# A windowed-attention and convolution kernel: buffers reused in the conv's tail, the next stage's first loads and table load placed among its last steps, and the depthwise taps loaded by channel

## The chip, the cores and the metric

The kernel runs on one core of a Trainium2 chip. A core has five engines, each with its own queue of instructions: TensorE (PE, matrix products), VectorE (DVE), ScalarE (ACT), GpSimd (POOL) and SyncE (SP, which here only issues transfers). ACT and POOL issue transfers too. The metric is the device time of one execution in microseconds (us); the median of several executions is compared.

## The reference

The input is `x`, 4 images of 128 channels and 128x128 pixels, fp32. Two layers follow one another.

```python
# layer 0
tok = regions(x)                     # 9x9 regions of 16x16 pixels, step 14, per image
y = ln(tok); q, k, v = split(y @ w_qkv)           # 4 heads of 32
o = softmax(q k^T / sqrt(32)) v
merged = overlap_average(o @ w_out + b_out + tok)
xf = merged.reshape(b, h * w, c)
y = ln(xf) @ w_p0 + b_p0                          # 256 channels
ym = depthwise_conv5x5(y, dw_k)                   # dw_k: [256, 1, 5, 5]
ym = batch_norm(ym)                               # statistics over all 4 images
y = gelu(gelu(ym)) @ w_p2 + b_p2 + xf
# layer 1
out = conv3x3(act_quant(y), weight_quant(w1)); out = batch_norm(out)
out = conv3x3(act_quant(out), weight_quant(w2)); out = batch_norm(out)
return out + y
```

The batch norms split the work: the gelu stage can't begin before the depthwise conv of the whole batch has its statistics.

## The kernel before, in words

**Stages.** The first, long stage (to about 2134 us) does attention, the first projection and the depthwise conv. Then comes the gelu stage (`gelu_stage`, L1228), which works through 64 units of 1,024 pixels: two gelus, second projection, residual, quantisation, first 3x3 conv. The second 3x3 conv (`last_stages`, L1354) ends the kernel.

**First stage.** An image is cut into 9 bands of regions, 36 bands in all; a band has 9 regions. For each region PE makes scores (L829), ACT exponentials (L837), DVE and POOL the sums `sm` of the two halves of the keys (L847), PE the weighted values (L892) and the sums (L900); DVE takes reciprocals (L912) and products `part` (L914, L916), and POOL adds regions into the band's output `ob` (L919). When a band is complete, `post_begin` (L545 to L557) averages the seams of `ob` on POOL; then `post_chunks` works on the band in chunks of 8 rows or fewer: the output projection (`product`, L473), the residual `xf` on DVE (`project`, L584), the second layer norm (squares L406, sums by PE L412, statistics L418 to L427), the first projection and its eviction `y` by ACT (L602), and stores of `y` to DRAM. The layer norm's row is spread over the partitions by a DRAM round trip (`xn<-row`, L446), except in the last band, where four selector matrices `sel` (made at L391) do it on PE (L439).

**Order.** PE, ACT, DVE and SP keep the order in which the program issues; POOL's instructions are placed by a scheduler and then run in order. `beside(t)` gives, for each of the 9 regions of band `t`, lists of small jobs of other bands. A list of single steps, `todo`, is dealt out over the first bands in the same way: it makes the matrices of the depthwise conv. The conv itself is a product with banded matrices: `zeros` loads the 25 taps of 256 channels as [25, 256] (L241), clears a scratch tile and stores it over `pad_d` in DRAM (L243), `padded_taps` writes the taps into it (L254), `by_outputs` reads bands out of it with a skewed pattern (L263), and later steps turn them and store them to `dw_d`. The second step after `padded_taps` is empty. When the list is done, `clear` (L322) zeroes the three input tiles `ut_` of the conv; the three weight tiles `wt_` are zeroed at the start. Their empty places stay zero after that.

**The conv.** `depthwise` (L640) multiplies weight tiles `w` (loaded from `dw_d`, L629) with input tiles `u` (loaded from `y2_d` by `fill`, L654: the main part by SP, two halo rows by POOL). Images 0 to 2 and the first half of image 3 are done beside the attention. The second half of image 3 is the tail: `conv_rest` (L733) runs 16 steps with a ring of six buffer pairs `ur`, `wr`, which it allocates and zeroes first (L750 to L757). It issues the weight loads and most of the input loads for six steps; after the last band's chunks, `run_all` loads the remaining rows and runs the steps. Each step has two results, which ACT copies out of PSUM (L769), DVE takes statistics of (L773), and SP and ACT store to `cv_d` (L776).

**Between the stages.** DVE and POOL work out scale and shift of the batch norm (`affine`, L1051). `gelu_stage` opens its pools, SP issues the loads of units 0 and 1 (`load` L1241 and L1246, `load_xf` L1255), and ACT runs the gelus (L1263, L1266), whose function table is loaded when the first of them comes up.

Of the kernel before, what the change touches and what calls it, by code (L numbers as in the profile page):

```python
# [14 lines left out]
P = 128  # L15
# [33 lines left out]
def layers(  # L49
# [135 lines left out]

    with ExitStack() as actx:
        pool = lambda name, bufs, **k: actx.enter_context(
            tc.tile_pool(name=f"{name}_{tag}", bufs=bufs, **k)  # L190
# [30 lines left out]
        def scratch(n):  # L221

            return turned(ut_)[:, :n]
# [6 lines left out]
        def band_matrices():  # L230

            held = {}

            def zeros():
                zero = scratch(28 * CW)
                nc.gpsimd.memset(zero, 0.0)
                held["taps"] = taps = scratch(2 * P)[:N_TAPS]  # L240
                nc.sync.dma_start(out=taps, in_=dw_k.rearrange("c o i j -> (o i j) c"))  # L241
                n = (2 * GR + 3) * 7 * 2 * P // P
                nc.sync.dma_start(  # L243
                    out=pad_d.rearrange("y x c -> (y x c)").rearrange("(p n) -> p n", p=P),
                    in_=zero[:, :n],
                )
                held["zero"] = zero

            def edge(b, m, n, g):
                nc.gpsimd.dma_start(  # L250
                    out=rows_in(b, g, m, n), in_=held["zero"][:, : n * CW].rearrange("p (n x) -> p n x", x=CW)
                )

            def padded_taps():  # L254
                for dy in range(5):
                    nc.sync.dma_start(
                        out=pad_d[GR - 1 + dy, 1:6, :], in_=held["taps"][5 * dy : 5 * dy + 5, :]
                    )

            def by_outputs(ro):  # L260
                for eo in range(2):

                    nc.sync.dma_start(  # L263
                        out=band_d[2 * ro + eo].rearrange("s (r e) c -> r s (e c)", e=2),
                        in_=bass.AP(
                            pad_d.tensor,
                            pad_d[GR - 1 - ro, 1 - eo, 0:1].offset,
                            [[7 * 2 * P, GR + 4], [4 * P, 3], [1, 4 * P]],
                        ),
                    )  # L270

            def load(c, s):
                by_m = scratch(32 * 64)[:KD].rearrange("p (m c) -> p m c", m=32)
                nc.sync.dma_start(
                    out=by_m, in_=band_d[:, s, :, c : c + 64].rearrange("m p c -> p m c")
                )
                held[c, s] = by_m

            def turn(c, s, half):
                if half == 0:  # L280
                    held["c"] = scratch(32 * 64)[:KD]
                by_m, by_c = held[c, s], held["c"]
                nc.vector.tensor_copy(
                    by_c[:, half * 1024 : half * 1024 + 1024].rearrange("p (c m) -> p m c", m=32),
                    by_m[:, :, 32 * half : 32 * half + 32],
                )
                if half:
                    del held[c, s]
                    h, k = divmod(c // 16, NCK)
                    for m, d in enumerate(dw_d):  # L290
                        n = d.shape[2] // 2
                        for jj in range(2):
                            nc.sync.dma_start(
                                out=d[k : k + 4, jj, n * h : n * h + n, 256 * s : 256 * s + 256].rearrange(
                                    "k p n -> p k n"
                                ),
                                in_=by_c[2 * GR * m : 2 * GR * m + n].rearrange(
                                    "p (k j n) -> p k j n", j=2, n=8 * 32
                                )[:, :, jj],
                            )  # L300

            def several(*steps):
                def run_all():
                    for s in steps:
                        s()
                return run_all

            each = lambda f, args: [lambda a=a: f(*a) for a in args]
            pieces = [(c, s) for c in range(0, 2 * P, 64) for s in range(3)]
            steps = [zeros, padded_taps, lambda: None]  # L310
            edges = [
                (b, 2 * GR * half + m, n, g)
                for b in range(B) for half in range(2)
                for m, n, g in ((0, 4, 0), (4, 4 if b == B - 1 else 28, NG - 1))
            ]
            for ro in range(GR):
                steps.append(several(*each(edge, edges[ro : ro + 1]), lambda ro=ro: by_outputs(ro)))
            steps += [lambda: None, lambda: load(*pieces[0])]

            def clear():  # L320
                for t in ut_:
                    nc.gpsimd.memset(t, 0.0)  # L322


            for n, p in enumerate(pieces):
                steps.append(
                    several(lambda p=p: turn(*p, 0), *each(load, pieces[n + 1 : n + 2]))
                )
                steps.append(lambda p=p: turn(*p, 1))
            steps.append(clear)  # L330
            return steps
# [398 lines left out]
                for half in range(2)  # L730
            ]

        def conv_rest(n, pool):  # L733

# [10 lines left out]
                U[at], W[at] = ring[at % ahead]  # L747
                weights(W[at], *tiles[at], nc.gpsimd.dma_start)

            ring = []  # L750
            for n_ in range(ahead):
                ring.append((
                    pool.tile([P, ng, 8, CW], F32, name=f"ur{n_}"), pool.tile([P, 3, 8, 32], F32, name=f"wr{n_}"),
                ))
                for t, engine in zip(ring[-1], (nc.vector, nc.gpsimd)):
                    engine.memset(t, 0.0)

            for at in range(ahead):
                begin(at)
# [3 lines left out]
            def step(at):  # L763
# [1 line left out]
                pc = score_banks(at, ng)  # L765
                depthwise(pc, W[at], U[at], 8)
                for half in range(2):
                    cv = pool.tile([P, 2, ng, CW], F32, name="cr", bufs=8)
                    nc.scalar.copy(  # L769
                        cv.rearrange("p j g x -> p (j g x)"), pc[half].rearrange("p j g x -> p (j g x)")  # L770
                    )
# [9 lines left out]
            def run_all():  # L781
# [3 lines left out]
                for at in range(len(tiles)):  # L785
                    step(at)
                    if at % 2:
                        chunk_stats(at // 2)
                    if at + ahead < len(tiles):
                        begin(at + ahead)  # L790
                        load(at + ahead, 0, ng)

            return run_all

# [213 lines left out]
        with nullcontext() if safe else tc.manual_schedule(engines=MANUAL):  # L1008
# [26 lines left out]
            post_begin(T - 1)  # L1035

            bctx.close()
            late = actx.enter_context(tc.tile_pool(name=f"late_{tag}", bufs=1))
            assert not todo
            run(left)  # L1040
            left.clear()
            flush(len(stores))
            rest = conv_rest(len(units) - 1, late)
            run(beside(T, selector(late.tile([P, 4 * P], F32, name="sel"))))
            flush(len(stores))
            rest()
# [139 lines left out]
        nc.gpsimd.memset(q[:, 1 : QW - 1, QW - 1 :], 0.0)  # L1186
        return q

    U = 2 * RB * P
    units = [(b, k) for b in range(B) for k in range(NU2)]  # L1190

    def pixels(k):
        return slice(k * U, (k + 1) * U)

    def rows_in(q, k):
        return q[:, 1 + 2 * RB * k : 1 + 2 * RB * (k + 1), 1 : 1 + P]
# [30 lines left out]

    def gelu_stage():  # L1228
        with (
            tc.tile_pool(name="ld", bufs=3) as ld,  # L1230
            tc.tile_pool(name="bw", bufs=2) as bw,
            tc.tile_pool(name="ps_b", bufs=2, space=PSUM) as ps_b,
            tc.tile_pool(name="ps_c", bufs=2, space=PSUM) as ps_c,
        ):
            loaded, stores = {}, []

            def load(n):
                b, k = units[n]
                cv = ld.tile([P, 2, U], F32, name="cv")
                if b < B - 1:  # L1240
                    nc.sync.dma_start(  # L1241
                        out=cv,
                        in_=cv_d[b][k // 2].rearrange("(h p) n -> p h n", p=P)[:, :, pixels(k % 2)],
                    )
                for h in range(2 if b == B - 1 else 0):
                    nc.sync.dma_start(  # L1246
                        out=cv[:, h],
                        in_=cv_d[b][k // 8, 32 * h : 32 * h + 32, k // 2 % 4, :, pixels(k % 2)],
                    )
                loaded[n] = [cv]  # L1250

            def load_xf(n):
                b, k = units[n]
                xf = ld.tile([P, U], F32, name="xfl")
                nc.sync.dma_start(out=xf, in_=xf_d[b][:, pixels(k)])  # L1255
                loaded[n].append(xf)

            def gelus(n):

# [40 lines left out]
                if b < B - 1:  # L1300
                    stores.append((c1_d[b][:, pixels(k)], c))

            for n in range(2):
                load(n)
            for n in range(2):
                load_xf(n)
            gelus(0)
            before1()
            before2()
# [23 lines left out]

    def last_stages():
        with (
            tc.tile_pool(name="fp", bufs=3) as fp,
            tc.tile_pool(name="zp", bufs=4) as zp,
            tc.tile_pool(name="idp", bufs=8) as idp,
            tc.tile_pool(name="ps_d", bufs=4, space=PSUM) as ps_d,
        ):  # L1340
            firsts, idt = {}, {}

# [111 lines left out]
```

## Time and profile before

| | |
|---|---|
| median of 3 executions | 3073.88 us (3073.38 to 3084.14) |
| the profiled execution, its own time | 3078.95 us |
| its span in the trace | 3077.1 us |
| mean granted clock of PE | 0.984 |
| DMA moved | 688.20 MB, 224 GB/s |
| packets, of them under 512 bytes | 748,167, of them 584,102 |

The engines' clocks in the trace count from the span's start. Three stretches matter for the change. From 150 to 230 us the first steps of `todo` run beside the second and third bands. From 2000 to 2134 us the last regions, the last band's chunks and `conv_rest` run. From 2134 to 2155 us the first stage gives over to the gelu stage.

The view of the waits, which lists by line what an engine waited for, shows this of PE at the output projection (waited us, times, the longest):

```
PE pm L473 <- DVE xf L584: 8.2, 1, 8.2
PE pm L473 <- POOL ob L557: 3.5, 1, 3.5
```

How to read the profile: a row of a group gives line, engine, operation, output and inputs with their shape, the count, then busy time and the mean in ns, then the idle time just before them with what ended it. A row of the chain of waits gives the start, the length and what held the last-ending chain of work at that moment. "issue" is time in which the engine waited for nothing that the profile shows. A slice of the page's rows of digits is 1/40 of the span, 77 us, and each digit tenths.

### The profile page before, as it was taken

Reading aid. Unit: us, or ns where it says so; the run is one execution under the profiler, and the core shown is the slowest. Engines: PE = TensorE matmul, PEld = TensorE weight load, DVE = VectorE, ACT = ScalarE, POOL = GpSimd, SP = SyncE. Lnnn points to the kernel's source line nnn. Section 1 sums busy time; section 2 is a strip of 40 time slices with the busy share of each in tenths; the row PEclk is TensorE's granted clock in tenths of the full one; section 3 lists DMA queues with packets and bytes.
Section 4 is the critical chain, followed back from the end, with each engine's and each line's share of the span. In section 5 each row is a group of like instructions: output and inputs, shape, how many; then the busy total and the mean of one; then the engine's idle time right before and its main releaser. Section 6 shows DMA issues by size and latency. Waiting matters only on the chain.

```text
span 3077.1 us, 88930 instructions
## 1 busy us (share of the span) xinstructions
PE 2963.6 (96%) x37626; PEld 1432.7 (47%) x37626; DVE 2029.1 (66%) x3186; ACT 1984.7 (64%) x2642; POOL 1020.6 (33%) x1370
## 2 busy tenths in 40 slices
PE   7999999999999999999999999976999999999998
PEld 4545554444444444444444445534444444444443
DVE  4867898777777677777676766654555555666543
ACT  5778787777777777777766766633767676333443
POOL 5444445444443444444344444343111111000000
PEclk9999999999999999999999999988999999999999
DMA  7455776777776677787698888879999997451498
GB/s 162 130 148 175 181 186 179 203 220 219 210 218 181 184 222 201 218 223 207 170 247 240 231 234 229 226 210 274 353 358 361 358 347 246 158 163 55 156 361 305
DMA packets 748167, 688.20 MB, mean 224 GB/s; under 512 B 584102, under 2 KB 622319, under 8 KB 740079
## 3 DMA queue, kind: packets, MB, share of 16 engines
q1 hardware_dynamic: 717391, 648.96, 70.5%
q0 software_dynamic: 12608, 28.74, 3.3%
q10 hardware_dynamic: 17760, 4.71, 0.7%
q8 instruction: 299, 4.90, 0.6%
q14 instruction: 109, 0.89, 0.1%
HBM read 410.68 MB, written 275.51 MB: 223 GB/s over the span
## 4 chain that ended last, share of the span: by engine, by line
PE 85%; DVE 5%; ACT 4%; DMA 3%; issue 2%; SPq 1%; ACTq 0%; POOL 0%; DVEq 0%
PE pc L1205 22%; PE pm L473 19%; PE pm L640 10%; PE sc L829 9%; PE po L892 9%; PE pb L1275 7%; PE po L900 4%; PE pm L412 3%; DVE rd L912 2%; PE sc L640 2%; ACT v L820 1%; DMA y_d<-y 1%; ACT pt L837 1%; DVE xn L456 1%; DVE xf L584 1%
## 5 line engine op out<-in xcount | busy, mean ns | idle before, releaser
L912 DVE RECIPROCAL rd<-po 128x256 f32<-128x256 f32 x324 | 568.8, 1756 | 373.8 <-PE po L900 369.0
L1205 PE MATMUL pc<-q,wq 128*128 128x512 fp8e4 x3168 | 700.6, 381 | 5.1 <-DVE q L1217 5.1
L837 ACT ACTIVATE pt<-sc 128x1024 f32<-128x1024 f32 x648 | 628.5, 1026 | 118.5 <-PE sc L829 58.9
L847 POOL TENSOR_TENSOR sm<-pt 128x512 f32<-128x512 f32 x324 | 414.8, 1280 | 665.6 <-ACT pt L837 484.1
L1205 PEld LDWEIGHTS <-wq 128*128 128x128 fp8e4 x3168 | 309.1, 98 | 406.8 <-issue 39.1
L829 PE MATMUL sc<-q,kr 32*128 32x256 f32 x5184 | 391.6, 403 | 20.6 <-ACT pt L837 19.7
L829 PEld LDWEIGHTS sc<-q,kr 32*128 32x128 f32 x5184 | 242.8, 184 | 272.7 <-issue 181.5
L892 PE MATMUL po<-pt,v 128*32 128x256 f32 x5184 | 352.7, 390 | 12.8 <-DVE part L916 12.4
L640 PE MATMUL pm<-u,w 64*32 64x504 f32 (+3 forms) x6144 | 313.5, 535 | 0.4 <-DVE xf L584 0.4
L847 DVE TENSOR_TENSOR sm<-pt 128x512 f32<-128x512 f32 x324 | 248.6, 767 | 23.5 <-ACT pt L837 23.5
L473 PE MATMUL pm<-xn,wqkv 128*32 128x512 f32 (+1 forms) x2304 | 246.7, 549 | 1.9
L473 PE MATMUL pm<-xn,wp 128*32 128x512 f32 (+1 forms) x2304 | 241.1, 549 | 3.0 <-DVE rstd L419 1.4
L1275 PE MATMUL pb<-cv,wp 128*128 128x512 f32 x512 | 232.5, 597 | 9.5 <-ACT cv L1266 9.5
L602 ACT ACTIVATE y<-pm,vectors 128x512 f32<-128x512 f32 (+1 forms) x288 | 182.8, 641 | 88.5 <-PE pm L473 52.5
L703 ACT COPY c<-pm 128x512 f32<-128x512 f32 x224 | 120.6, 590 | 184.5 <-PE pm L640 177.9
L892 PEld LDWEIGHTS po<-pt,v 128*32 128x32 f32 x5184 | 138.6, 110 | 178.8 <-issue 86.9
L1213 DVE BATCH_NORM_STATS2 st<-pc 128x6 f32<-128x512 f32 x256 | 165.8, 690 | 84.9 <-PE pc L1205 84.9
L919 POOL TENSOR_TENSOR ob<-ob,part 128x32 f32<-128x32 f32 x288 | 129.0, 448 | 234.8 <-DVE part L916 227.5
L900 PE MATMUL po<-sm,ones 128*32 128x256 f32 x2592 | 204.0, 384 | 0.0
L707 DVE BATCH_NORM_STATS2 st<-c 128x6 f32<-128x512 f32 (+1 forms) x256 | 146.0, 617 | 83.7 <-ACT c L703 83.5
L1287 POOL TENSOR_SCALAR a<-y 128x1024 f32<-128x1024 f32 x64 | 66.5, 1039 | 398.9 <-DVE y L1283 398.9
L640 PEld LDWEIGHTS pm<-u,w 64*32 64x32 f32 x6144 | 110.4, 106 | 161.7 <-issue 125.9
(165 smaller groups left out, 3735.2 us busy)
## 6 DMA issues: line engine op xcount, KB each, us to landing
cv_d<-c SPq DMA_DIRECT2D x224, 256.0 KB
u<-y_d SPq DMA_DIRECT2D x96, 560.0 KB
cv<-cv_d SPq DMA_DIRECT2D x48, 1024.0 KB
xn<-row SPq DMA_DIRECT2D x76, 512.0 KB
y_d<-y SPq DMA_DIRECT2D x136, 256.0 KB
xfl<-xf_d SPq DMA_DIRECT2D x64, 512.0 KB
id_d<-y SPq DMA_DIRECT2D x64, 512.0 KB
idt<-id_d SPq DMA_DIRECT2D x64, 512.0 KB
```

The source lines that it names most:

```text
L473: nc.tensor.matmul(out[m], w[:, m], v, start=True, stop=True)
L602: nc.scalar.activation(y[:, :n], pm[:, : n * P].rearrange("p (r c e) -> p r e c", r=n, e=2), AF.Identity, bias=bp0[:, h : h + 1],)
L640: nc.tensor.matmul(outs[half][32 * q : 32 * q + 32, j, :, a:z], wt[hs, s, c, :], ut[hs, :, c, a + s - 1 : z + s - 1], start=(s == 1), stop ...
L829: nc.tensor.matmul(sc[h // 2][:, h % 2, kc, :].rearrange("p (r c) -> p r c", c=RS), region(kr, j)[hs, kc * P : (kc + 1) * P], queries(j, h ...
L837: nc.scalar.activation(pt, sc[p], AF.Exp)
L847: add(sm, pt[:, :, 0, :], pt[:, :, 1, :], ALU.add)
L892: nc.tensor.matmul(po[hs, 0, :], v[:, kc, hs], pt[h // 2][:, h % 2, kc, :], start=(kc == 0), stop=(kc == 1),)
L900: nc.tensor.matmul(po[hs, 1, :], ones, sm[h // 2][:, h % 2, :], start=True, stop=True)
L912: nc.vector.reciprocal(rd, po[:, 1, :])
L1205: nc.tensor.matmul(pc[:, h], w[:, t, :], q1[b][:, r + dy : r + dy + RB, dx : dx + P], start=(t == 0), stop=(t == 8),)
L1213: nc.vector.bn_stats(st[:, 2 * n + h, :], pc[:, h])
L1275: nc.tensor.matmul(pb[:, m], wp2[:, h, :], cv[:, h, px], start=(h == 0), stop=(h == 1))
```

## The change

Four edits stand in the diff.

1. **The ring of `conv_rest`.** The first three of the six pairs are the main conv's tiles `ut_` and `wt_`, seen in the ring's shape. Three new pairs are allocated, and POOL zeroes both members of each. The result buffers `cr` go from 8 to 7.
2. **The gelu stage's first loads and table.** The pool `ld` is opened before `conv_rest`; `load` and `load_xf` move out of `gelu_stage`, and units 0 and 1 are loaded after step 12 of 16. After the last step ACT runs one gelu on a [128, 1] tile.
3. **Waits by tile.** The pools of the tail and of the later stages take `reuse_waits="tile"`: a tile waits for what used its own memory, not for the whole of a closed pool.
4. **The taps.** `zeros` loads `dw_k` as [128, 2, 25], by channel. A new step, `turned_taps`, transposes it with two products on PE and a copy on DVE; it takes the slot of `padded_taps`, which takes the empty slot behind it.

```diff
             def zeros():
                 zero = scratch(28 * CW)
                 nc.gpsimd.memset(zero, 0.0)
-                held["taps"] = taps = scratch(2 * P)[:N_TAPS]
-                nc.sync.dma_start(out=taps, in_=dw_k.rearrange("c o i j -> (o i j) c"))
+                held["rows"] = rows = scratch(2 * N_TAPS).rearrange("p (h t) -> p h t", h=2)
+                nc.sync.dma_start(out=rows, in_=dw_k.rearrange("(h p) o i j -> p h (o i j)", p=P))
...
+            def turned_taps():
+                held["taps"] = taps = scratch(2 * P)[:N_TAPS]
+                pm = ps_m.tile([P, 2, P], F32, name="pm")[:N_TAPS]
+                for h in range(2):
+                    nc.tensor.transpose(pm[:, h], held["rows"][:, h], ident)
+                nc.vector.tensor_copy(taps, pm.rearrange("p h c -> p (h c)"))
...
-            steps = [zeros, padded_taps, lambda: None]
+            steps = [zeros, turned_taps, padded_taps]
...
-        def conv_rest(n, pool):
+        def conv_rest(n, pool, next_loads):
...
-            ring = []
-            for n_ in range(ahead):
+            ring = [
+                (t[:, : ng * 8 * CW].rearrange("p (g c x) -> p g c x", g=ng, c=8), w) for t, w in zip(ut_, wt_)
+            ]
+            for n_ in range(ahead - len(ring)):
                 ring.append((
                     pool.tile([P, ng, 8, CW], F32, name=f"ur{n_}"), pool.tile([P, 3, 8, 32], F32, name=f"wr{n_}"),
                 ))
-                for t, engine in zip(ring[-1], (nc.vector, nc.gpsimd)):
-                    engine.memset(t, 0.0)
+                for t in ring[-1]:
+                    nc.gpsimd.memset(t, 0.0)
...
-                    cv = pool.tile([P, 2, ng, CW], F32, name="cr", bufs=8)
+                    cv = pool.tile([P, 2, ng, CW], F32, name="cr", bufs=7)
...
+                    if at == len(tiles) - 4:
+                        next_loads()
+                warm = pool.tile([P, 1], F32, name="warm")
+                nc.scalar.activation(warm, eps_t, AF.Gelu)
...
-            late = actx.enter_context(tc.tile_pool(name=f"late_{tag}", bufs=1))
+            late = actx.enter_context(tc.tile_pool(name=f"late_{tag}", bufs=1, reuse_waits="tile"))
+            ld.append(lctx.enter_context(
+                tc.tile_pool(name=f"ld_{tag}", bufs=3, side="right", reuse_waits="tile")
+            ))
...
-            rest = conv_rest(len(units) - 1, late)
+            rest = conv_rest(len(units) - 1, late, first_loads)
...
-            for n in range(2):
-                load(n)
-            for n in range(2):
-                load_xf(n)
             gelus(0)
```

`load` and `load_xf` keep their text; what calls them is now

```python
    def first_loads():
        for n in range(2):
            load(n)
            load_xf(n)
```

In the built order, the loads of unit 2, which `gelu_stage` issues in its loop, stand on SP ahead of the tail's last two stores.

## The prediction

> **What bounds the kernel now.** I read the page's totals, its slices, and the chain of work that ended last; then that chain, the groups and the waits in the stretches where TensorE (PE) is not full.
>
> ```profile
> PE 2963.6 (96%) x37626; PEld 1432.7 (47%) x37626; DVE 2029.1 (66%) x3186; ACT 1984.7 (64%) x2642; POOL 1020.6 (33%) x1370
> ...
> PE   7999999999999999999999999976999999999998
> ...
> PEclk9999999999999999999999999988999999999999
> ...
> PE 85%; DVE 5%; ACT 4%; DMA 3%; issue 2%; SPq 1%; ACTq 0%; POOL 0%; DVEq 0%
> ```
>
> PE is busy 96% of the span and is 85% of the chain: the kernel is bound by its matmuls, and none of them is removed. An edit can only recover time in which PE is idle, or slow after idling. The slices show one such place: numbers 27 and 28 (2000 to 2154 us), where PE falls to 7 and 6 tenths and its clock to 8. A slice is 77 us, so short stalls hide in it; the chain finds another, near 155 us:
>
> ```profile
> 155.25 0.70 SPq L241
> ...
> 156.00 8.76 SPq L243
> ...
> 164.86 4.04 DMA xn<-row
> ```
>
> Columns: start, length, what held the chain. The queue of SyncE (SP) stands 8.76 us at line 243, the store behind the tap load of line 241, and the rows that PE needs next can only be asked for at 164.86. The tail:
>
> ```profile
> 2024.19 1.76 DVE ur L756
> ...
> 2034.89 1.76 DVE ur L756
> ...
> 2036.94 0.66 DVE xf L584
> ...
> 2037.64 1.94 PE pm L473 x8
> ...
> 2044.72 5.41 PE pm L439 x16
> ...
> 2127.19 3.68 PE sc L640 x123
> ...
> 2132.00 3.32 DMA cv_d<-cr
> ...
> 2135.40 7.02 DMA cv<-cv_d
> ...
> 2143.04 1.28 ACT L1263
> ...
> 2144.34 1.53 ACT cv L1263 x2
> ```
>
> VectorE (DVE) clears buffers at line 756 for 12.5 us while line 584, which takes results of PE, stands behind them; and from the conv's last matmuls to the first gelu there are a store, a load and a table load.
>
> **Part 1: the taps.** Removed: a load of 6,400 single elements. Added: a load of 256 rows of 100 bytes, two transposes on PE, one copy on DVE. What the old load costs is read from the spacing of equal work: the score matmuls of that region start at 126.01, of the next band's at 178.95, of the one after at 224.54, so this band took 52.94 us and its neighbour 45.59: 7.35 us lost. What remains: SP issues the load where it does now, about 155.25, but the transposes follow the output matmuls that end about 155.4 in PE's order, so PE itself now waits for a load just issued, behind the 384 KB image load of 154.86. Such image loads landed 3.2 us after issue (197.44 to 200.67 in the chain). The row load is not in the trace: from below, PE waits 2 us; from above, as long as the old load (10.9 us from 155.25 to the landing, a loss of 2.8 on balance). I take 3.2, the near row. Two transposes at 0.27 (the 128x128 products of line 473 take 274 ns) add 0.55; the copy (0.36, as the 128x512 copy of line 391) runs on DVE beside PE. Sum: −7.35 + 3.75 = **−3.6**, ends −5 and +2.8.
>
> **Part 2: the ring of buffers.** Six clears leave DVE, three of them for good; three go to the Pool engine (POOL), which loses three clears of `wr`:
>
> ```profile
> L756 DVE MEMSET ur<- 128x2048 f32 x6 | 10.6, 1765 | 2.7 <-issue 1.9 <-POOL ob L919 0.8
> L756 POOL MEMSET wr<- 128x768 f32 x6 | 4.2, 729 | 0.0
> ```
>
> On DVE, line 584 could start at 2027.6 (the output products start at 2026.65) and started at 2036.94: 9.3 us are freed. But POOL gives part of it back, since those products wait for its work on `ob` (lines 554 to 557). A clear of 128x2240 on POOL takes 1.965 us (line 322), so one of 2048 takes 1.80: 3 x 1.80 − 3 x 0.73 = +3.2 us. In the program's order, POOL also gets the loads of `w` and the halos of the three reused buffers (0.56 us an issue, line 654) ahead of its last region sums. Two groups of four fit: POOL is free at 2003.15 and needed at 2003.47, free at 2012.95 and needed at 2012.70. The rest push the last addition into `ob` from 2023.4 to about 2026, and two halo issues and a `w` issue then stand between the three operations on `ob`: their end moves from 2026.6 to about 2030, **+3.5**.
>
> So PE, idle 3.5 us there now (2023.1 to 2026.6), would idle 6.8. Here the Trainium skill speaks against the change ("TensorE: Matmul & The Clock Gate", Part 1: after an idle window of about 3.4 us PE runs at half rate, and needs as long to recover). The rows:
>
> ```profile
> 2028.00:2032.00 4.00, 1.43 (x16) 0.22 (x8) 3.25 (x3) 0.00 (x0) 4.00 (x7) 0.97 0.74 248
> 2032.00:2036.00 4.00, 0.00 (x0) 0.00 (x0) 3.25 (x3) 0.00 (x0) 3.47 (x7) 0.50 0.98 316
> ...
> 2096.00:2100.00 4.00, 1.37 (x53) 0.89 (x38) 2.85 (x13) 1.07 (x2) 3.15 (x6) 1.00 1.15 346
> ...
> 2120.00:2124.00 4.00, 3.66 (x135) 2.70 (x124) 2.31 (x11) 1.07 (x2) 0.00 (x0) 1.00 0.76 154
> ```
>
> (Windows: busy us with counts of PE, weight loads, DVE, ACT, POOL; granted clock; DMA share; GB/s.) After the present 3.5 us the 24 output matmuls still ran fast (2.78 us); after 7 us idle the clock is 0.50, and eight products take 1.94 instead of 0.9. By the row of 3.5 us the chunk's sums would end some 8 us earlier; by the rule, the longer idle makes the four groups of products end at 2035.8, line 584 at 2036.6 instead of 2040.4, and the sums (line 412) at 2038.9 instead of 2043.4: −4.5. I take the rule, as the 0.50 row bears it out. The selector products of line 439, cold now, may save up to 1.7 of their 5.41 when PE comes to them warm; I count 0.5. Stores, landings and halo loads after them shift along: DMA is nearly idle from 2046 to 2052, so no load takes their place. Sum: **−5**, ends −8 and −1.
>
> **Part 3: early loads and the gelu table.** The loads of the first units follow conv step 12 (in the built order those of the third unit too, before SP's last two stores). Now the first gelu waits for a load issued at 2135.40 and landed at 2142.42, then for a table load of 1.28, and starts at 2144.34. With both done, it waits for the batch norm's scale and shift, ready at 2139.64: **−4.65** if free. It isn't: about 4.5 MB now arrive while the conv ends. The conv shows what traffic does to it. Its matmuls come in blocks of about 125, each followed by a gap that the chain calls issue. At a DMA share of 1.13 to 1.16 (2075 to 2118) blocks start every 6.15 us, seven of them; at 0.75 every 4.1 to 4.6, with gaps of 0.34 to 0.88. The page has 299 packets of 4.90 MB in queue q8, "instruction": 16.4 KB each, which is about 256 instructions, 128 matmuls with their weight loads. The skill has the rule for such refills ("Runtime: NRT & Kernel Launch", Instruction fetch mechanics): blocks of 16 KiB, their cost mostly hidden by prefetch. By the rule the gain stays −4.65; by the rows, the last block, from 2127.19, is late as the saturated ones are, by 1.5 to 2, and an earlier one may be too (+5 at most). I take the rows, +2: **−2.65**, ends −4.65 and +0.5. The gelus and products behind then run at their own pace (7.34 us a step from 2157.9) and shift along; POOL's clears of the padded tiles (done 2147.1, needed after 2150) stay covered, by 0.4 us at least.
>
> **Part 4: waits by tile, 7 `cr` buffers.** At the changes of stage PE waits for no pool in the trace: the one at 2610 to 2627 ends on a DVE shift, and the last stage's loads are hidden by some 440 us of continuous products. Seven buffers still hold three steps of stores, which land in 3.3 us. **0**, cover lost only if a store takes over 15 us.
>
> **Sum.** −3.6 − 5 − 2.65 = −11.2: on the profiled execution 3078.95 − 11.2 = 3067.7. That one lies 5 us above the median of the runs shown, to which no stall found here belongs; the forecast in their frame is 3073.88 − 11.2, about **3063**.
>
> **Rivals.** *All costs hidden* (0.26): the rows land within 2 us, PE stays fast before the products, fetches hide: −5 − 8 − 4.65 = −17.7, **3056**. For it: each part then does what its removed stall allows; against it: the clock of 0.50 and the 6.15 us blocks.
> *Gains handed on* (0.2): POOL's delay eats DVE's gain, the conv ends as much later as gelu starts earlier; −3 from the taps, −1 from the ring: **3070**. For it: the products wait for `ob` by POOL already now (3.5 us in the table of waits).
> *POOL's queue stalls* (0.06, slower): POOL executes in order, so a `w` load that waits for an earlier one holds the region sums behind it. If the eight issues of each hoisted group take 2 us each in place of 0.56 (5.8 us twice), and the late ones delay the end of `ob` by 6 more, parts 1 and 3 are outweighed: about +7, **3081**. It decides from 14 us of such waits. Against it: the margins above, and buffers whose earlier loads landed long before.
>
> **Numbers.** Forecast 0.48. About 0.5% (15.4 us) is what a measurement here can tell from no change. The range holds from the first rival's far end and execution noise (the three runs differ by 10.8) to the handed-on case: 3051 to 3074. Faster than 3058.5: most of the first rival and the forecast's lower edge, 0.36; slower than 3089: 0.05; between: 0.59.
>
> **What would show it.** Taps: the band spaced 52.94 comes down to about 49.3, no 8.76 at SP, PE waiting some 3 us for the row load. Ring: `ob` complete about 3.5 us later (after the shift of part 1), no DVE clears after it, the conv's first matmul 5 us earlier. Loads: last blocks near 6 us apart, no table load after the conv, first gelu right after the shift. A conv that starts later than now, or a POOL issue of over 1 us in front of a region sum, would prove me wrong.

## The result, and the profile after

The changed kernel took 3066.99 us (median of 8 runs, 3064.04 to 3074.75), the kernel before 3078.94 in the runs beside it. The ratio is 0.9967, 95% interval 0.9951 to 0.9982: some 10 us, between 5.5 and 15. A second set of runs gave 0.9967 again (0.9956 to 0.9979). The forecast was 11.2 us. Its absolute figure, 3063, was counted from a median of three runs, 3073.88, that proved 5 us below the one here. (One of the eight runs of the kernel before, of 4610 us, was slow and is left out of the ratio.) The profiled execution has a span of 3064.6 us, 12.5 below that of before.

From the page of the changed kernel, totals and the shares of the chain:

```profile
PE 2953.6 (96%) x37628; PEld 1425.3 (47%) x37628; DVE 2019.5 (66%) x3181; ACT 1985.5 (65%) x2643; POOL 1023.6 (33%) x1370
...
PE 83%; DVE 5%; DMA 4%; ACT 4%; issue 3%; SPq 1%; POOL 1%; ACTq 0%; DVEq 0%; POOLq 0%
```

PE has two matmuls more (the transposes) and is 10 us less busy: much of the saved time is time in which PE ran slow, not only time in which it stood. DVE has five operations fewer. POOL has 1% of the chain. The digits of the slices are those of before, 7 and 6 tenths in the same two. The chain near 155 us and in the tail (start, length, what held it):

```profile
156.01 3.28 DMA u<-in_L_conv_dw_k_dram
...
159.34 0.62 PE pm L291 x2
...
2023.87 0.43 POOL ob L597
...
2024.35 6.04 PE pm L513 x32
...
2034.69 3.72 PE pm L479 x16
...
2051.34 2.33 DMA u<-y_d
2053.67 10.96 PE sc L680 x276
...
2131.53 1.52 ACT cv L1287 x2
```

The 8.76 us of SP are gone, and PE itself waits for the row load. No clear by DVE stands in the tail; PE waits for POOL's last operation on `ob`, and then runs its 32 output products in 6.04 us. The windows (columns as before) show that those products ran at half clock, with POOL busy throughout, and the groups what POOL's clears take:

```profile
2024.00:2028.00 4.00, 3.65 (x20) 0.99 (x24) 0.75 (x1) 0.00 (x0) 4.00 (x8) 0.50 1.09 261
```

```profile
L798 POOL MEMSET ur<- 128x2048 f32 x3 | 5.4, 1804 | 0.0
```

The conv starts at 2053.67 instead of 2065.27, the first gelu at 2131.53 instead of 2144.34. The table load still comes behind the conv's end (2126.47, by ACT's timeline), but ahead of the wait for the batch norm, so it costs nothing here. Ahead of the conv PE waits for a halo load as long as before (8.2 us, 8.1 before): what is won further ahead reaches the conv in full.

Cut at the same instructions (starts of the score matmuls in PE's timeline), the two profiled executions differ so: start to third band +0.8 us, third band −2.6, fourth band to the last region −2.3, from there to the conv's first matmul −7.5, conv to the first gelu −1.2, the rest +0.3; together −12.5. Nothing in the first of these stretches nor in the long one was changed, so 2 to 3 us of such a difference are chance, and a single trace can't be the judge of terms of that size. The experiments therefore serve twice: each is a trial of its own, and its untouched stretches repeat those of the others. Their stretches in us, and the ratio of their time to that of the kernel before:

| kernel | to 3rd band | 3rd band | last scores to conv | conv to 1st gelu | ratio |
|---|---|---|---|---|---|
| before | 126.0 | 52.9 | 55.3 | 79.1 | |
| new taps alone | 123.8 | 52.0 | 53.9 | 80.1 | 1.0004 |
| new ring alone | 127.8 | 51.7 | 49.3 | 78.7 | 0.9989 |
| changed | 126.8 | 50.3 | 47.8 | 77.9 | 0.9967 |
| changed, again | 125.0 | 50.6 | 47.7 | 77.3 | 0.9967 |
| loads free to move | 128.7 | 51.9 | 50.9 | 77.2 | 0.9973 |
| loads at the gelu stage | 125.4 | 50.5 | 49.1 | 77.9 | 0.9965 |
| `ur` cleared by DVE | 123.9 | 52.1 | 47.5 | 74.3 | 0.9958 |
| weights by SP | 125.4 | 50.5 | 48.1 | 79.2 | 0.9980 |
| loads after the last step | 124.8 | 50.6 | 49.2 | 73.6 | 0.9964 |
| empty step added | 129.3 | 46.0 | 48.4 | 76.8 | 0.9968 |
| that, DVE clears, loads last | 132.1 | 46.0 | 46.3 | 75.3 | 0.9961 |
| taps grouped | 127.8 | 45.8 | 49.2 | 76.3 | 0.9961 |
| grouped, DVE clears, loads last | 128.1 | 45.8 | 47.9 | 73.9 | 0.9946 |

All that lies between (fourth band to last region) took 1828.7 to 1840.9 us in these executions, with no order that the edits explain. That is why the ratios, with intervals of about 0.0012 to either side (4 us), tell less than the stretches. The experiments ran on four chips, on which the kernel before took 3076.4, 3082.4, 3081.4 and 3083.3 us in the median; each ratio is taken on one chip, but the stretches are compared across them.

### The profile page after: what moved, and what is told of

Same layout as the page of the kernel before. It is cut to its first block, busy times and chain, and to the rows that moved or that the text cites. A ratio compares the mean times of both kernels' runs of the same rounds, so it can differ in the third digit from the quotient of the medians.

```text
span 3064.6 us, 88932 instructions
## 1 busy us (share of the span) xinstructions
PE 2953.6 (96%) x37628; PEld 1425.3 (47%) x37628; DVE 2019.5 (66%) x3181; ACT 1985.5 (65%) x2643; POOL 1023.6 (33%) x1370
## 4 chain that ended last, share of the span: by engine, by line
PE 83%; DVE 5%; DMA 4%; ACT 4%; issue 3%; SPq 1%; POOL 1%; ACTq 0%; DVEq 0%; POOLq 0%
PE pc L1250 22%; PE pm L513 18%; PE pm L680 9%; PE sc L875 9%; PE po L938 9%; PE pb L1299 7%; PE po L946 4%; PE pm L452 3%; DVE rd L958 2%; DMA y_d<-y 2%; PE sc L680 1%; ACT pt L883 1%; ACT v L866 1%; DVE xn L496 1%; DMA xn<-row 1%
```

## The experiments

**New taps alone**, on the kernel before: the hunks of `zeros`, `turned_taps` and `steps`.

> The kernel before, with the new load of the taps alone. Theory (each edit acts in its own stretch and the sums add): the region scores of the third band to those of the fourth come down from 52.9 us by 2.6, as in the changed kernel, with PE waiting some 3 us for the row load; the tail as before (last region's scores to the conv's first matmul 55.3 us, conv 65.6 us); time 2 to 4 us below before. Rival (the drift of 2.3 us that the changed kernel shows between 230 and 2000 us belongs to this edit): that stretch is shorter here too, and the time is 5 us below.

Ratio 1.0004 (0.9996 to 1.0012): the part gains nothing that a time shows, at most 1.2 us where the theory gave 2 to 4. Its third band takes 52.0 us, one less than before instead of 2.6. The rival falls too: the stretch from the fourth band to the last region was 3 us longer, not shorter. The transposes wait 3.0 us, as in the changed kernel, but PE runs slow for longer behind them: the spacing of the two regions around them is 9.74 us, against 9.03 in the changed kernel and 4.23 without them.

**New ring alone**, on the kernel before: the hunks of the ring and its clears.

> The kernel before, with the reused tiles in the ring and all clears on POOL; pools wait as before, 8 result buffers. Theory: the ring alone brings the whole gain of the tail: last region's scores to the conv's first matmul 47.8 us instead of 55.3, the work on ob done some 18.5 us after those scores (16.6 before), the conv itself as before (65.6 us); time 7 us below before. Rival (the waits by tile carry part of it, since the clears on POOL then wait for the pools that close): ob done 3 us later than that, 50 to 51 us, and time 3 to 4 below.

Ratio 0.9989 (0.9979 to 0.9998), 3 us: the time is the rival's, not the theory's 7. The trace is nearer to the theory: 49.3 us from the last scores to the conv, 6 less than before, and `ob` done 18.5 us after the scores as in the changed kernel: POOL made its clears at the same places, so the waits of pools take nothing from it, and the rival's cause falls. Why the time shows less than the stretch stays open. PE ran the output products in 5.55 us and the selectors in 5.41, cold. Its third band, with the old taps, took 51.7 us: so what the old load costs varies too, 6.2 us here and 7.4 before (the band after it takes 45.5 in every trace).

**Loads free to move.** From the changed kernel:

```diff
-                    if at == len(tiles) - 4:
-                        next_loads()
-                warm = pool.tile([P, 1], F32, name="warm")
-                nc.scalar.activation(warm, eps_t, AF.Gelu)
...
+            first_loads()
             gelus(0)
```

> The changed kernel with the loads of the first two units back at the start of the gelu stage and no gelu on the small tile. Theory (the loads are what lengthens the conv): the conv takes 65.6 us again instead of 69.0, from its end to the first gelu 13.5 instead of 8.9; net 1.2 us slower than the changed kernel, 11 us below before. Rival (the longer conv comes from the ring, as its first three buffers are freed late, or from chance): the conv stays near 69, and the time is 4.6 us above the changed kernel.

It wasn't the experiment I meant. The pool `ld` still waited by tile, so nothing held the loads, and they were placed earlier instead of later. SP's timeline (start, length, instruction):

```profile
2032.22 0.50 SPq L199 DMA_DIRECT2D cv<-cv_d  x1
...
2057.00 0.52 SPq L213 DMA_DIRECT2D xfl<-xf_d  x1
```

ACT's timeline of the same run:

```profile
2131.84 1.28 ACT L1283 ACT_TABLE_LOAD   x1 [0.43 <-ACT cr L811]
2139.12 1.52 ACT L1283 ACTIVATE cv<-cv,shift,scale 128x512 f32<-128x512 f32 x2 [6.00 <-DVE shift L1102]
```

Yet it teaches something: the first gelu again waits for the batch norm only, and the table load came ahead of that wait with no small gelu to call it. The wait by tile alone sets the loads free; the hand-made placing decides only where they go. Here they stood among the last band's stores, and the conv began 50.9 us after the last scores, the latest of all with the new ring. Its conv took 68.3 us, though all these loads were issued by 2074: a conv as long as the changed kernel's 69.0 is no sign, by itself, of loads among its last steps.

**Loads at the gelu stage**, with a pool opened there that waits for whole pools:

```diff
-            lctx,
+            tc.tile_pool(name="ld", bufs=3) as ld_,
...
+            ld.append(ld_)
+            first_loads()
             gelus(0)
```

(and without the four lines taken out above, and without the pool opened ahead of `conv_rest`).

> The changed kernel with the pool of the loads opened in the gelu stage again, waiting for whole pools, the loads behind it, and no gelu on the small tile. Theory (the early loads gain 4.65 us after the conv and cost some of it within): conv's end to the first gelu 13.5 us instead of 8.9; the conv 65 to 66 us if the loads are what made it 69.0, and then the time is 1 to 2 us above the changed kernel. Rival (the length of the conv varies by itself, as 64.0 us with early loads in the run with clears on DVE suggests): the conv anywhere from 64 to 69, and the time 4 to 5 us above the changed kernel in the median.

From the conv's end to the first gelu 13.1 us, the conv 64.9. Together 77.9, which lies 0.7 above the changed kernel's second execution and at its first. The ratio, 0.9965 (0.9955 to 0.9976), shows no loss. The early loads where the change puts them are worth about 2 us at most.

**The changed kernel once more.**

> The changed kernel once more, to see how far its stretches differ between two profiled executions. If the stretches are steady: third band 50.3, last region's scores to the conv's first matmul 47.8, conv 69.0, conv's end to the first gelu 8.9 us, each within 0.5. If the row load's landing and the conv's length are chance: third band up to 52, conv 64 to 69.

Third band and start of the conv repeat within 0.4 us. The conv does not: 65.1 us instead of 69.0, and then 12.1 instead of 8.9 to the first gelu. The sum hardly moves (77.3 and 77.9). ACT's timeline says what took the place of the late last block (idle before, and what ended it, in brackets):

```profile
2115.95 1.07 ACT L811 COPY cr<-sc 128x512 f32<-128x512 f32 x2 [1.59 <-PE sc L680]
2121.28 0.37 ACTq L818 DMA_DIRECT2D cv_d<-cr  x1
2121.77 1.07 ACT L811 COPY cr<-sc 128x512 f32<-128x512 f32 x2 [4.74 <-DMA xfl<-xf_d]
```

ACT's second store of the step before the last is issued only when the load of the first `xf` has landed: the trace names that landing as what ended the wait. Neither data nor buffer ties the two. The semaphores in the packed trace do: the store waits for number 104, which the load of `xf` raises when it lands and which the store then takes over. The issues of SP and ACT in this stretch share eight such numbers, used in turn. The last step's copies stand behind it, and its statistics and the batch norm behind those. The wait was 4.1 us with the empty step, 6.1 with the weights by SP, 3.0 with DVE's clears (so 3.0 to 6.1 in the four traces, where the next expectation says 4.1 to 6.1).

**Loads after the last step.** From the changed kernel:

```diff
-                    if at == len(tiles) - 4:
+                    if at == len(tiles) - 1:
```

> The changed kernel with the first loads after the last conv step (16 of 16) instead of after step 13. Theory (the early loads gain less than they remove because ACT's store of the step before the last waits for the landing of the load of xf, 4.1 to 6.1 us in four traces, and the last eviction, its statistics and the batch norm stand behind it): no wait of ACT for a load of xf, conv's end to the first gelu 8.9 to 10 us with the conv at 65 to 66, so 74 to 75.5 us from the conv's first matmul to the first gelu instead of 77.2 to 77.9; time 2 to 3 us below the changed kernel. Rival (now the first gelu waits for its load, which takes 7 us as before): 77 us or more, and no gain.

The wait is gone, as ACT's timeline shows:

```profile
2120.38 1.07 ACT L811 COPY cr<-sc 128x512 f32<-128x512 f32 x2 [2.02 <-PE sc L680]
2121.48 0.37 ACTq L818 DMA_DIRECT2D cv_d<-cr  x1
2122.94 1.08 ACT L811 COPY cr<-sc 128x512 f32<-128x512 f32 x2 [1.49 <-PE sc L680]
...
2131.73 1.52 ACT L1287 ACTIVATE cv<-cv,shift,scale 128x512 f32<-128x512 f32 x2 [5.76 <-DVE shift L1106]
```

The conv took 64.7 us and the first gelu followed 8.9 after it: 73.6, some 4 less than in the changed kernel, and in the two other kernels that have this edit 75.3 and 73.9. The first gelu did not wait for its load, issued at 2123.96; the rival falls. The margin is small: that load landed at 2131.21, by its semaphore, and the gelu began at 2131.73. The time alone (0.9964, 0.9951 to 0.9977) doesn't tell 3 us.

**`ur` cleared by DVE.** From the changed kernel:

```diff
-                for t in ring[-1]:
-                    nc.gpsimd.memset(t, 0.0)
+                for t, engine in zip(ring[-1], (nc.vector, nc.gpsimd)):
+                    engine.memset(t, 0.0)
```

> The changed kernel with the three new ur tiles cleared by DVE instead of POOL; the wr tiles stay on POOL. Theory (POOL's queue is what PE waits for before the output products): ob is done about 2 us earlier than in the changed kernel, while DVE is busy with the clears for 6.2 us after the last region's product and holds the fourth group of output products by 1 to 2 us; the conv's first matmul within 2 us of the changed kernel, most likely 1 earlier. Rival (DVE is the tight one): the conv's first matmul 4 us or more later than in the changed kernel, as three of the six clears are back.

`ob` is done 15.6 us after the last scores instead of 18.5, PE waits 2.5 us for it instead of 5.3, and the fourth group of products waits 0.7 for DVE. The conv starts 0.3 us earlier than in the changed kernel; over the three kernels with these clears 47.2 on average, against 48.7 over the seven with POOL's clears and weights (the ring alone, changed twice, loads at the gelu stage, loads last, empty step, grouped). So about 1.5 us, which is the theory's direction (46.3 to 47.9 against 47.7 to 49.3, so the two sets overlap at the edge). The ratio, 0.9958 (0.9943 to 0.9974), includes 74.3 us from the conv to the first gelu, which nothing in this edit explains.

**Weights by SP.** From the changed kernel, in `begin`:

```diff
-                weights(W[at], *tiles[at], nc.gpsimd.dma_start)
+                weights(W[at], *tiles[at], nc.sync.dma_start if at < ahead else nc.gpsimd.dma_start)
```

> The changed kernel with the weight loads of the first six conv steps issued by SP instead of POOL. Theory (seven transfers issued by POOL stand between its clears and the end of ob, 0.5 us each, and PE idles cold behind them): ob is done 2.5 us earlier, PE's idle time before the output products falls from 5.3 to about 2.7 us, the 32 products take 3.7 instead of 6.0 us as PE stays at its clock; last region's scores to the chunk's sums 23 instead of 27.5 us; time 4 us below the changed kernel. Rival (SP now reaches the stores of y later, and conv's loads collide with them): the sums come earlier but the conv's first matmul does not.

POOL's timeline:

```profile
2022.79 1.11 POOL L694 DMA_DIRECT2D ur<-y_d  x2
2023.90 1.27 POOL L694 DMA_DIRECT2D u<-y_d  x2
2025.16 0.55 POOL L694 DMA_DIRECT2D ur<-y_d  x1
2025.74 0.26 POOL L965 TENSOR_TENSOR ob<-ob,part 128x32 f32<-128x32 f32 x1
```

The scheduler filled the places of the weights with halo loads that it had placed behind `ob` before. `ob` came 0.6 us earlier instead of 2.5, the products ran cold all the same (6.48 us), and the time is 0.9980 (0.9971 to 0.9989), no gain over the 0.9967 of the changed kernel beside it. Whether POOL's transfers cost PE that wait is left undecided by this run; the run with DVE's clears speaks for POOL's queue.

**An empty step ahead of the transposes.**

```diff
-            steps = [zeros, turned_taps, padded_taps]
+            steps = [zeros, lambda: None, turned_taps, padded_taps]
```

> The changed kernel with one empty step between zeros and turned_taps, so that the transposes come a region later in PE's order. Theory (PE's wait for the row load has eaten the gain of the taps: 4.8 to 6.1 us in the traces with the new load, against 6.2 to 7.4 us lost with the old one): PE waits under 0.5 us, the third band takes 46 to 46.5 us instead of 50.3 to 52.1, and the time is 4 to 6 us below the changed kernel. Rival (the wait only moves, to the writes of the taps on SP or to the band's rows behind it): the third band stays above 49 us, and the time is that of the changed kernel.

The third band takes 46.0 us: the wait is gone, not moved behind. But the time is 0.9968 (0.9957 to 0.998), that of the changed kernel: the stretch is the theory's, the time the rival's. In this trace a loss stands ahead of the band, where neither had put it: the third band begins at 129.3 us, later than in any kernel with the old list (123.8 to 128.7).

**The same with DVE's clears and the loads last.**

> The changed kernel with three of the edits tried: one empty step ahead of the transposes of the taps, the new ur tiles cleared by DVE, the first loads after the last conv step. Theory (the gains stand in different stretches and add): third band 46, last region's scores to the conv's first matmul 47.5, first matmul to first gelu 74 to 75.5 us; time 7 to 9 us below the changed kernel, ratio to the kernel before about 0.994. Rival (PE's saved time in the third band is lost in a later band to transfers that come no earlier, as the equal times with and without the empty step suggest): the third band is 46 but the time is only 3 us below the changed kernel.

Ratio 0.9961 (0.9948 to 0.9974), some 2 us below the changed kernel where the theory gave 7 to 9 and the rival 3. The three stretches are near the theory's, but the third band begins at 132.1 us. The view of the waits from 70 to 92 us:

```profile
DVE am L390 <- DMA u<-in_L_conv_w_dram: 8.0, 1, 8.0
PE po L938 <- DVE part L962: 8.0, 2, 7.6
```

The list of steps also quantises the weights of the 3x3 convs, ahead of `zeros`. With one step more it is dealt out anew, and the reduction `am` came up on DVE one region earlier than in the changed kernel, ahead of that region's reciprocal, while its load (issued at 63 us, 15 us to landing) was still on its way: DVE waits 8.0 us and PE behind it (6.5 and 6.1 with the empty step alone). In the twelve traces with the old list, where `am` comes a region later, it waits for 0 to 4.3 us (0 and 0.8 in the two of the changed kernel).

**Taps grouped**, the list kept at its length:

```diff
-            steps = [zeros, turned_taps, padded_taps]
+            steps = [zeros, lambda: None, several(turned_taps, padded_taps)]
```

> The changed kernel with the list of steps kept at its length: an empty step after zeros, then turned_taps and padded_taps in one step. Theory (in the run with an added empty step the whole list was dealt out anew, and a DVE step of the second band came up a slot earlier, before its load had landed; that took back the 4.5 us won in the third band): the first two bands take 124 to 127 us as in the changed kernel, not 129 to 132, the third 46 to 46.5, and the time is 4 to 5 us below the changed kernel, ratio to the kernel before about 0.995. Rival (the gain of the third band is given back by work behind it): the third band is 46, but the time stays at 0.9967.

The third band takes 45.8 us, almost as the one behind it, and begins at 127.8, inside what kernels with the old list show (123.8 to 128.7) but at its upper end: `am` waited 4.3 us by itself in this execution. The ratio, 0.9961 (0.9947 to 0.9975), lies 2 us below that of the changed kernel and can't be told from it.

**Grouped, DVE's clears, loads last.**

> The same with the new ur tiles cleared by DVE and the first loads after the last conv step. Theory: third band 46, last region's scores to the conv's first matmul 46.5 to 47.5, conv's end to the first gelu 8.9; 6 to 8 us below the changed kernel, ratio 0.994. Rival (DVE's clears and the later loads bring nothing that an execution shows): as the run with the grouped steps alone, 0.995.

Ratio 0.9946 (0.9933 to 0.9959), the lowest of all. The third band takes 45.8 us and the first gelu follows the conv's end by 8.9, as foretold; the middle stretch, 47.9, lies just above the 46.5 to 47.5. That is some 16 us below the kernel before (13 to 21), and 6 below the changed one, though the two intervals still overlap. It is the version that I would keep.

## Why the prediction was right, step by step

The sum, −11.2, met the measured −10 to −12, though an interval of 5.5 to 15 us would have taken in many sums. Its terms did less well: as the traces measure them they add to −9.2, with one larger than foretold and two smaller, so a part of the agreement is luck. The sizes below are means over all traces with and without the step, which are less open to chance than the pair of profiled executions.

- **The taps: −3.6 foretold, −1.3 measured** (third band 52.9 and 51.7 with the old load, 51.1 on average over the eight with the new one in the next step). The mechanism is as foretold, PE waits for the row load. The term that was too small is that wait: foretold 3.2 plus 0.55 for the transposes, in the traces 4.8 to 6.1 together. The load landed in 3.28 us in the changed kernel's chain, as the row of the image loads said; but PE, after 3 us idle, ran the transposes in 0.62 us and the 16 products behind them in 3.01, against 1.90 in the kernel before. I counted the idle time and not the slow time after it, though I had counted just that in the tail. The windows of the changed kernel and of the new taps alone, with the granted clock at 0.50, show how long PE was slow:

```profile
158.72:162.13 3.41, 2.79 (x14) 0.76 (x18) 1.04 (x3) 0.23 (x1) 0.63 (x1) 0.50 0.67 214
```

```profile
155.63:162.45 6.82, 6.03 (x34) 1.98 (x34) 1.13 (x4) 2.07 (x3) 0.63 (x1) 0.50 0.34 111
```

Five traces have the short kind there, and a third band of 50.3 to 50.6 us; three have the long kind (new taps alone, loads free to move, DVE's clears), and 51.9 to 52.1. What the old load took is 6.2 us in another trace; the 7.35 of the forecast should read 7.4, as the scores of the next band start at 224.47 and not at 224.54.

- **The ring: −5 foretold, −5.9 measured** (54.6 us over two traces, 48.7 over seven). DVE's clears are gone from the chain, and POOL gives part of it back by its clears and transfers. That term was foretold as +3.5 and is +1.8: counted from the last scores, the last addition into `ob` came 1.5 us later instead of 2.6, and the issues between the operations on `ob` added 0.3 instead of 0.9. The rule of the clock that the forecast took from the Trainium skill ("TensorE: Matmul & The Clock Gate", Part 1: half rate after an idle window of about 3.4 us) held where it was taken: after 5.3 us idle the 32 products took 5.5 to 6.0 us in the traces counted here, against about 3.7 at the rate of before (24 in 2.78). Pauses of 2.5 and 3.5 us did not all follow it, as the last section tells. (The row of 0.50 from which the forecast took it stood behind a pause of 8.2 us in the kernel before, not 7.) In the rival *all costs hidden* PE stays fast there; that part of it falls.
- **The early loads: −2.65 foretold, −2.0 measured** (79.0 us over the four traces with the loads at the gelu stage, 77.0 over the six with them after the thirteenth step, which is `at` = 12). The amount given back, 2.7, is near the 2 foretold; its place was only half right. A last block of the conv that comes late, 6.41 us after the one before, is in the first trace and in that of the grouped taps; in the second the conv ran through, and there and in three others ACT's store waited for a landing instead. I had counted the traffic and not the queue that the loads are moved ahead of. With the loads last the full −4.7 is there (74.3 us over three traces; two of them have DVE's clears too, the one without them shows 73.6), which the forecast had as the lower end.
- **Waits by tile and seven buffers: 0 foretold, not shown.** No run has them alone. In the stretches nothing speaks against 0, and POOL's clears stand at the same places with and without them. But the times do not add up: the new taps and the new ring alone gain 2 us together, the changed kernel 10, and without its early loads still 11. Some 8 us, give or take 5, belong to neither part alone nor to the early loads. The waits by tile are one candidate, chance and the parts' effect on each other are others. What is shown is that they let the loads go early at all, by the run with free loads.
- **The rivals.** *All costs hidden*, 17.7 us, and *gains handed on*, 4 us, both lie outside the interval of 5.5 to 15. What was handed back was in good part the taps' gain, which the latter had left standing. *POOL's queue stalls* falls: no issue of POOL ahead of a region sum took more than 0.6 us in the changed kernel's trace, and the conv starts earlier after the last scores in every trace with the new ring. (Its sum is for four issues in each group, not eight.)

What stays open: where those 8 us are, why DVE's clears came with the short 74.3 us, and how much of the first bands' 124 to 128 us is owed to the landing of the weight loads.

## What to carry to other kernels

When a load is made cheaper, ask who waits for it now: PE, which had stood idle, ran slow afterwards, so a wait of 3 us cost 5. A transfer moved forward also comes ahead of whatever waits for it in turn, on other engines too; the cheapest place here was right behind the last issue that mattered, not as early as could be. And where steps are dealt out from a list, an added step moves all of them: keep the length, and look at the stretches ahead of the edit as well as behind it.

## What was not expected of the hardware

The same pause doesn't always slow PE alike. Before the output products it was idle 3.5 us in the kernel before and in that with the new taps alone; 24 products then took 2.78 us in the one and 4.07 in the other. After 2.5 us, in the run with DVE's clears, they took 4.48, and after 2.4, in the run that adds the empty step and the late loads, 2.78. The granted clock changes in steps: in all traces of this case the stretches at half rate near the taps and in the tail lasted 3.41 us or a whole multiple of it. The selectors ran in 3.72 us in eight traces and in 5.41 in six, with the same 1.35 us ahead of them, and in all six a stretch of 3.41 us at half rate lay over them. It fits this that a pause counts by where it falls against the steps; no run here varied that alone. Some 1 to 2 us of the difference between two executions come from there.
